# Second sequence's modulation rows, modulation sums and routing logits on TensorE: three small rearrangements in an adaptive-norm attention and expert kernel

## The chip, the cores and the metric

The kernel runs on one core of one Trainium2 chip. Its engines are TensorE (PE; PEld is its weight load), VectorE (DVE), ScalarE (ACT), GpSimd (POOL) and SyncE (SP), which issues most of the DMAs. Each works through its own queue in order. The metric is device time in microseconds, the median of three executions.

## The reference, cut to what matters

The input holds two sequences of 1024 tokens with 512 features. A vector c of each sequence makes six modulation rows; normed and modulated tokens go through an attention with cosine similarities, then through a top-2 mixture of eight experts with a shared expert.

```python
mod = (_silu(L0_c) @ L0_wmod).reshape(2, 6, 1, -1)
sa, ca, ga, sb, cb, gb = (mod[:, i] for i in range(6))
ga = (2 * (ga >= 0) - 1) * jnp.maximum(jnp.abs(ga), 0.25)   # gb alike
h = _layernorm(x) * (1 + ca) + sa
x = x + ga * attention(h)     # layernorm, K, V, rotary, A = sum(cos(K) * cos(V)), (A * Q) @ W_out
h = _layernorm(x) * (1 + cb) + sb
x = x + gb * moe(h)           # scores = softmax(h @ gate_w), the best 2 of 8, shared expert
```

## The kernel before, in words

All values are fp32. Tokens are taken in tiles of 128 rows: tiles 0 to 7 are the first sequence, 8 to 15 the second. Four tiles make a group; there are four groups.

**Modulation rows.** `c` is turned into four column pieces `sc_pad` (128 features by 32 columns, two of them used). `mod_parts(m, w, t)` multiplies each of the four pieces with its 128 rows of weight m, in four column tiles of the array, so that the four partial sums lie in partitions 0, 32, 64 and 96 of one PSUM bank, two rows each; a ScalarE copy brings the bank to SBUF. The partial sums are added by one more product with `pick`, a 128x2 matrix that has a one where a partition belongs to a sequence. `mod_sum` does that for both sequences at once, into two rows of a bank; `mod_add` then adds a constant, `mod_gate` makes the gate (sign and magnitude; two VectorE rows, one ScalarE row and one more VectorE row), and both store the rows in DRAM (`mods`), from where `spread` reads them into all partitions. `spread_now` instead multiplies with one column of `pick` broadcast to 128 columns, so that the row of one sequence comes out on all partitions at once, and ScalarE copies it. So `ca1[0]`, `sa[0]` (first sequence) and `ca1[1]`, `sa[1]` (second) are made. `turn_mod` transposes the rows of cb and sb into columns, `modT`, which `turn2` uses much later.

**The opening.** Three filler products (`turn_over(3, ones_row)`) run while the first weights land; then come the parts of ca and sa, their rows for the first sequence, and four more filler products `turn_over(4, parts_sa)` until the first tile is normed.

**The loop over tiles 0 to 7.** For each tile t: `norm1(t + 2)` norms a tile two ahead (`norm1_in`: moments `st_a`, `mv`, `sd_a`, `rs`; `norm1_mid` and `norm1_out`: two VectorE rows on `h`, which has one buffer; moments `st_b`, `mv_b`, `sd_b`, `rs_b`, `off_b`; ScalarE writes `hn`). `kv_half(t, 0)` multiplies K (four products into a bank, which VectorE adds a bias to), `turn1(t + 1)` transposes the next tile (`tr_a`) and ScalarE copies it in four pieces to `xnT`; then the steps in `side[t]` run, then `kv_half(t, 1)` multiplies V and `kv_back` computes the cosine sums (`sq` on ScalarE, `pr`, `inv`, `w` and `acc` on VectorE, the rotation on GpSimd). `side` spreads the rest of the modulation work and the transposes of W_q (`turn_wq`, four banks `wqT_0` to `wqT_3`) over the tiles:

```python
0: [second_rows],
2: [lambda: mod_gate(2, wm_ga), turn_wq],
4: [lambda: add(4, wm_cb, 1.0), lambda: add(3, wm_sb, 0.0)],
5: [lambda: own(5, wm_gb), lambda: turn_mod(0, raws[4])],
6: [lambda: mod_gate(5, wm_gb), lambda: turn_mod(1, raws[3])],
```

After the loop `mix` sums `acc` over the tokens (`amix`), and the second sequence's loop runs among the output projections of the first.

**The logits.** For each group, `logit_parts` multiplies the four pieces of the gate weights (32 columns each, eight used) with the transposed tokens in four column tiles, again with four partial sums in partitions 0, 32, 64 and 96. `route` then adds them: for each of the four token tiles a product with `pick_e` (128x8), 128 tokens by 8 experts, and one VectorE copy of 128x32 to SBUF. The softmax and the choice of two experts follow on VectorE and ScalarE; `place_rows` multiplies ranks from it.

**Order.** PSUM has eight banks: three buffers for products (`mm_ps`), two for transposes and small products (`tr_ps`), three for the shared expert (`sh_ps`). The source's order is a proposal: a scheduler settles the order of the instructions in each engine's queue by its own estimate of times. `tc.issue_after(x)` keeps what stands in it behind instruction x.

Of the kernel before, what the change touches and what calls it, by code (L numbers as in the profile page):

```python
# [8 lines left out]
FP = mybir.dt.float32  # L9
# [3 lines left out]
ALU = mybir.AluOpType  # L13
AX = mybir.AxisListType
# [4 lines left out]
P = 128  # L19
# [5 lines left out]
def kernel(  # L25
# [20 lines left out]
    nc = tc.nc  # L46
    B, S, D = x.shape
    E, _, H = w_gate.shape
    KC = D // P
    CT = P // KC  # L50
# [29 lines left out]
    const = ctx.enter_context(tc.tile_pool(name="const", bufs=1))  # L80
# [30 lines left out]
    ident = const.tile([P, P], FP, name="ident")  # L111
# [3 lines left out]
    ones_t = const.tile([P, P], FP, name="ones_t")  # L115
# [75 lines left out]
    wm_ga = load_mod(2, 3)  # L191
# [4 lines left out]
    wm_cb = load_mod(4, 4)  # L196
    wm_sb = load_mod(3, 5)
# [6 lines left out]
    wm_gb = load_mod(5, 0)  # L204
# [17 lines left out]
    silu = nc.vector.tensor_mul(sc_pad[:, :, 0:B], csb, sig_c)  # L222
    pick = late.tile([P, B], FP, name="pick")
    with tc.issue_after(silu.ins):
        nc.vector.tensor_reduce(
            pick, ident.rearrange("p (k c) -> p c k", k=KC)[:, 0:B, :], AX.X, ALU.add
        )
    pick_e = const.tile([P, E], FP, name="pick_e")
    with tc.issue_after(silu.ins):
        nc.vector.tensor_reduce(  # L230
            pick_e, ident.rearrange("p (k c) -> p c k", k=KC)[:, 0:E, :], AX.X, ALU.add
        )
    parts = {}

    copied = []
# [11 lines left out]
            )  # L247
        copied.append(nc.scalar.copy(t, ps))

    def mod_sum(m, w):  # L250
        ps = mm_ps(f"modsum_{m}")
        nc.tensor.matmul(ps[:B, :], pick, w[:, 0, :], start=True, stop=True)
        return ps[:B, :]


    def mod_add(m, w, plus):
        t = w[:B, 1, :]
        nc.vector.tensor_scalar(t, mod_sum(m, w), plus, None, ALU.add)
        nc.sync.dma_start(mods[m], t)
        return t  # L260

    def mod_gate(m, w):

        ps = mod_sum(m, w)
# [15 lines left out]
        mod_parts(m, w, t)  # L280
        return t

    def spread_now(t, b, plus, tag):
        ps = mm_ps(f"{tag}_{b}")
        nc.tensor.matmul(
            ps, pick[:, b : b + 1].to_broadcast([P, P]), t, start=True, stop=True
        )
        row = late.tile([P, D], FP, tag=tag, bufs=B, name=f"{tag}_{b}")
        nc.scalar.activation(row, ps, AF.Identity, bias=plus)
        return row  # L290

    modT = late.tile([P, 2, KC, B], FP, name="modT")

    def turn_mod(i, raw):
        ps = tr_ps(f"modT_{i}")
        for f in range(KC):
            nc.tensor.transpose(
                ps[:, f * B : (f + 1) * B], raw[:, f * P : (f + 1) * P], ident[0:B, 0:B]
            )
# [27 lines left out]
    def transposes(src, name):  # L327
        ps = tr_ps(f"tr_{name}")
        for f in range(KC):
            nc.tensor.transpose(  # L330
                ps[:, f * P : (f + 1) * P], src[:, f * P : (f + 1) * P], ident
            )
        return ps
# [7 lines left out]
    hn_of, turned1 = {}, {}  # L341
# [37 lines left out]
    def turn1(t):  # L379
        g, j = t // 4, t % 4  # L380
        hn = hn_of.pop(t)
        if j == 0:
            xnT[g] = act_tile(XNT_HOME[g], f"xnT_{g}")
        ps = transposes(hn, f"a{t}")
        for f in range(KC):
            turned1[t] = nc.scalar.activation(  # L386
                xnT[g][:, f, j * P : (j + 1) * P],
                ps[:, f * P : (f + 1) * P],
                AF.Identity,
                bias=colsb[:, 1, f : f + 1],  # L390
                scale=colsb[:, 0, f : f + 1],
            )
# [219 lines left out]
    rows = const.tile([P, NT, TOPK], I32, name="rows")  # L612
# [32 lines left out]
    def route(g, lgp):  # L645

        t0 = g * 4
        ps = tr_ps(f"lg_{g}")
        for j in range(4):
            nc.tensor.matmul(  # L650
                ps[:, j * E : (j + 1) * E],
                lgp[:, j * P : (j + 1) * P],
                pick_e,
                start=True,
                stop=True,
            )
        lg = small.tile([P, 4, E], FP, tag="lg", name=f"lgs_{g}")
        nc.vector.tensor_copy(lg.rearrange("p j e -> p (j e)"), ps[:, 0 : 4 * E])
        mx = small.tile([P, 4], FP, tag="mx", name=f"mx_{g}")
        nc.vector.tensor_reduce(mx, lg, AX.X, ALU.max)  # L660
        nc.vector.tensor_sub(lg, lg, mx.unsqueeze(2).to_broadcast([P, 4, E]))
        ex = small.tile([P, 4, E], FP, tag="ex", name=f"ex_{g}")
        nc.scalar.activation(ex, lg, AF.Exp)
        sm = small.tile([P, 4], FP, tag="sm", name=f"sm_{g}")
        nc.vector.tensor_reduce(sm, ex, AX.X, ALU.add)
        nc.vector.reciprocal(sm, sm)
        p = small.tile([P, 4, E], FP, tag="p", name=f"p_{g}")
        nc.vector.tensor_mul(p, ex, sm.unsqueeze(2).to_broadcast([P, 4, E]))
# [17 lines left out]
        both = small.tile([P, 4, E], FP, tag="both", name=f"both_{g}")  # L686
        nc.vector.tensor_add(both, pick[:, :, 0, :], pick[:, :, 1, :])
# [366 lines left out]
        return kvp.tile([P, D + 2 * R2], FP, tag="acc", bufs=1, name=f"acc_{b}")  # L1054

    def second_rows():
        ca1[1] = spread_now(parts_ca, 1, ones_t[:, 0:1], "ca1")
        sa[1] = spread_now(parts_sa, 1, zero_t, "sa")

    def own(m, w):  # L1060
        mod_parts(m, w, w[:, 0, :])

    raws = {}

    def add(m, w, plus):
        raws[m] = mod_add(m, w, plus)


    side = {
        0: [second_rows],  # L1070
        1: [lambda: own(2, wm_ga)],
        2: [lambda: mod_gate(2, wm_ga), turn_wq],
        3: [lambda: own(4, wm_cb), lambda: own(3, wm_sb)],
        4: [lambda: add(4, wm_cb, 1.0), lambda: add(3, wm_sb, 0.0)],
        5: [lambda: own(5, wm_gb), lambda: turn_mod(0, raws[4])],
        6: [lambda: mod_gate(5, wm_gb), lambda: turn_mod(1, raws[3])],
        7: [lambda: before_mix(0)],
    }
    turn_over(3, ones_row)
    parts_ca = own_parts(1, wm_ca)  # L1080
# [4 lines left out]
    parts_sa = own_parts(0, wm_sa)  # L1085
    norm1_mid(0)
    sa[0] = spread_now(parts_sa, 0, zero_t, "sa")
    turn_over(4, parts_sa)
    norm1_in(2)
    norm1_out(0)  # L1090
    norm1_mid(1)
    turn1(0)
    norm1_out(1)
    acc = start_acc(0)
    for t in range(NJ):
# [486 lines left out]
    sums = list(range(NT))  # L1582
# [106 lines left out]
```

## Time and profile before

| | |
|---|---|
| three executions | 773.6, 773.07, 772.42 us, median 773.07 |
| profiled execution | 773.89 us, span 772.0 us |
| busy: TensorE, VectorE, ScalarE, GpSimd | 754.5, 427.8, 233.3, 211.7 us |
| mean granted TensorE clock | 0.997 of full speed |

A row of the timeline has the start in microseconds from the span's beginning, the duration, engine, line and operation, the tensors written and read (buffer numbers left out), shapes, and the number of instructions merged; in brackets stands how long the engine had been idle and what ended it. A row of the waits has the engine and what it was about to do, whom it waited for, the total in microseconds, the number of times and the longest. An fp32 product of 512 columns appears as two records of 0.43 us spacing, a transpose of 128x128 as one.

### The profile page before, as it was taken

The page shows a single profiled execution, that of the slowest core. Times are in us where ns is not written, and L with a number is a line of the kernel's source. Part 1 is how long each engine was busy: PE and PEld are TensorE (multiplying, and loading weights), DVE is VectorE, ACT ScalarE, POOL GpSimd, SP SyncE. Part 2 cuts the span into 40 slices and gives each one's busy share as a digit, 9 for nine tenths or more (in the row PEclk, how much of TensorE's full clock was granted, in tenths as well). Part 3 has the DMA queues.
Part 4 walks back from the last instruction along what each step waited for, and adds up shares of the span by engine and source line. Part 5 has one row for each costly group of instructions (what it writes and reads, how often), then busy time and mean ns, then how long its engine had stood idle before and what let it go on. Part 6 is the DMA issues. An engine that isn't in the chain of part 4 may idle for free. (4 is left out here: it accounts for less than half of the span.)

```text
span 772.0 us, 8521 instructions
## 1 busy us (share of the span) xinstructions
PE 754.5 (98%) x2547; PEld 418.6 (54%) x2547; DVE 427.8 (55%) x980; ACT 233.3 (30%) x496; POOL 211.7 (27%) x241
## 2 busy tenths in 40 slices
PE   7999999999999999999999999999999998999997
PEld 2444444444444444584565656656656554888542
DVE  4888856898736888882221223222221121499964
ACT  4565523567542153110122111122111111122310
POOL 1234324754632686562100000000000000234530
PEclk9999999999999999999999999999999999999999
DMA  8951001312515611367999999999999885524551
GB/s 320 382 170 29 1 1 68 122 54 73 158 65 193 262 68 42 119 262 254 343 352 357 335 339 327 331 349 322 342 321 326 303 279 169 191 83 134 166 164 54
DMA packets 96368, 158.91 MB, mean 206 GB/s; under 512 B 8088, under 2 KB 51096, under 8 KB 96320
## 3 DMA queue, kind: packets, MB, share of 16 engines
q1 hardware_dynamic: 89984, 138.41, 53.3%
q0 software_dynamic: 5760, 18.88, 7.3%
q10 hardware_dynamic: 576, 1.05, 0.4%
q8 instruction: 22, 0.36, 0.2%
q14 instruction: 26, 0.21, 0.1%
HBM read 128.15 MB, written 30.16 MB: 205 GB/s over the span
## 5 line engine op out<-in xcount | busy, mean ns | idle before, releaser
L1341 POOL DMA_INDIRECT y<-ybuf,yrows x32 | 36.9, 1154 | 336.1 <-SPq L1567 287.0
L403 PE MATMUL kv<-w_kv,xnT 128*128 128x512 f32 x256 | 115.0, 596 | 0.5 <-ACT xnT L386 0.5
L1467 PE MATMUL by<-wd_r,gtT 128*128 128x512 f32 (+1 forms) x210 | 96.1, 593 | 0.9 <-DVEq L1559 0.9
L1439 PE MATMUL bg<-wg_r,hbT 128*128 128x352 f32 x280 | 88.9, 460 | 0.9 <-ACT y L1471 0.9
L1439 PE MATMUL bu<-wu_r,hbT 128*128 128x352 f32 x280 | 88.5, 459 | 0.0
L403 PEld LDWEIGHTS kv<-w_kv,xnT 128*128 128x128 f32 x256 | 47.0, 190 | 57.4 <-issue 49.0
L1439 PEld LDWEIGHTS bu<-wu_r,hbT 128*128 128x128 f32 x280 | 53.2, 190 | 29.6
L1454 DVE COPY gtT<-gtr 128x256 f32<-128x256 f32 x35 | 14.8, 424 | 97.0 <-PE gtr L1451 97.0
L1439 PEld LDWEIGHTS bg<-wg_r,hbT 128*128 128x128 f32 x280 | 50.4, 190 | 23.5 <-ACT y L1471 1.3
L564 PE MATMUL o<-wp,xnT 128*128 128x512 f32 x128 | 57.3, 593 | 0.0
L1318 DVE TENSOR_TENSOR sg_b<-sg_b,bg 128x352 f32<-128x352 f32 x35 | 18.2, 521 | 68.7 <-ACT sg_b L1317 68.7
L1467 PEld LDWEIGHTS by<-wd_r,gtT 128*128 128x128 f32 (+1 forms) x210 | 37.2, 191 | 34.6 <-issue 33.5
L1431 ACT COPY hbT<-tr_b 128x512 f32<-128x512 f32 x36 | 21.1, 585 | 101.2 <-PE tr_b L330 101.2
L1319 DVE TENSOR_TENSOR gt<-sg_b,bu 128x352 f32<-128x352 f32 x35 | 18.2, 521 | 47.2 <-PE bu L1439 47.2
L1471 ACT COPY y<-by 128x512 f32<-128x512 f32 x35 | 20.5, 587 | 70.8 <-PE by L1467 45.0
L564 PEld LDWEIGHTS o<-wp,xnT 128*128 128x128 f32 x128 | 23.9, 190 | 28.6 <-issue 27.0
L1317 ACT ACTIVATE sg_b<-bg 128x352 f32<-128x352 f32 x35 | 16.2, 463 | 76.1 <-PE bg L1439 76.1
L433 POOL TENSOR_TENSOR cross<-kv 128x128 f32<-128x128 f32 x16 | 12.6, 789 | 75.6 <-DVE kv L410 44.0
L426 ACT ACTIVATE sq<-kv 128x512 f32<-128x512 f32 x32 | 20.1, 630 | 31.1 <-DVE kv L410 26.7
L523 PE MATMUL wp<-aw,wqT 128*128 128x512 f32 x64 | 28.6, 597 | 0.9 <-DVE aw L504 0.7
L603 POOL TENSOR_TENSOR hr<-hr,cb 128x512 f32<-128x512 f32 x16 | 22.3, 1395 | 23.8 <-issue 13.2
L386 ACT ACTIVATE xnT<-tr_a,colsb 128x128 f32<-128x128 f32 x64 | 24.2, 456 | 14.2 <-PE tr_a L330 14.2
(320 smaller groups left out, 1269.2 us busy)
## 6 DMA issues: line engine op xcount, KB each, us to landing
wg_r<-in_w_gate_dram SPq DMA_DIRECT2D x35, 704.0 KB, 6.5
wu_r<-in_w_up_dram SPq DMA_DIRECT2D x35, 704.0 KB, 7.7
wd_r<-in_w_down_dram SPq DMA_DIRECT2D x35, 512.0 KB, 5.6
hb<-hbuf SPq DMA_DIRECT2D x36, 256.0 KB, 5.2
ybuf<-y SPq DMA_DIRECT2D x31, 256.0 KB, 5.4
wd_r<-in_w_down_dram SPq DMA_DIRECT2D x35, 192.0 KB, 5.6
wmod<-in_wmod_dram SPq DMA_DIRECT2D x6, 1024.0 KB, 10.5
x<-in_x_dram SPq DMA_DIRECT2D x3, 1024.0 KB, 10.5
```

The source lines that it names most:

```text
L386: turned1[t] = nc.scalar.activation(xnT[g][:, f, j * P : (j + 1) * P], ps[:, f * P : (f + 1) * P], AF.Identity, bias=colsb[:, 1, f : f + 1 ...
L403: nc.tensor.matmul(ps, xnT[g][:, k, j * P : (j + 1) * P], w_kv[:, i, k, :], start=(k == 0), stop=(k == KC - 1),)
L426: nc.scalar.activation(sq, kv[:, i, :], AF.Square, accum_out=ss[:, i : i + 1])
L523: nc.tensor.matmul(ps, wqT[:, k, f * P : (f + 1) * P], aw[:, k, :], start=(k == 0), stop=(k == KC - 1),)
L564: nc.tensor.matmul(ps, xnT[g][:, k, j * P : (j + 1) * P], wp[:, k, :], start=(k == 0), stop=(k == KC - 1),)
L603: nc.gpsimd.tensor_mul(h, h, cb1[b])
L1318: nc.vector.tensor_mul(sg[:m, :n], sg[:m, :n], pg[:m, :n])
L1341: nc.gpsimd.indirect_dma_start(out=y, out_offset=None, in_=ybuf, in_offset=bass.IndirectOffsetOnAxis(ap=yrows[:, t, s : s + 1], axis=0), b ...
L1431: nc.scalar.copy(hbT.rearrange("p k q -> p (k q)"), ps)
L1439: nc.tensor.matmul(ps[:, :H], hbT[:, k, :], wt[:, k, :], start=(k == 0), stop=(k == KC - 1))
L1467: nc.tensor.matmul(ps, gtT[:m, c, :], w[2][:m, c, :], start=(c == 0), stop=(c == NH - 1))
L1471: nc.scalar.copy(y, ps)
```

## The change

1. The products of the second sequence's rows `ca1[1]` and `sa[1]` move to the opening, in place of two of the four filler products; their copies on ScalarE are issued behind the last `xnT` copy of tile 0. `side[0]` becomes empty.
2. The sums of cb, sb and gb are multiplied in tile 5 into three column tiles of one bank (partitions 0, 32 and 64); the sum of ga stays alone in tile 2. The parts of gb move from tile 5 to tile 4, the gate of gb from tile 6 to tile 5, the stores of cb and sb from tile 4 to tile 5, the transpose of cb from tile 5 to tile 6.
3. The partial logits are transposed as they are, four 128x128 transposes for each group, and VectorE adds the four partial sums as it reads the bank. `pick_e` goes.

```diff
-    pick_e = const.tile([P, E], FP, name="pick_e")
...
-    def mod_sum(m, w):
-        ps = mm_ps(f"modsum_{m}")
-        nc.tensor.matmul(ps[:B, :], pick, w[:, 0, :], start=True, stop=True)
-        return ps[:B, :]
+    def mod_sums(*ws):
+        ps = mm_ps("modsums")
+        sums = []
+        for i, w in enumerate(ws):
+            rows = slice(i * CT, i * CT + B)
+            nc.tensor.matmul(
+                ps[rows, :], pick, w[:, 0, :], start=True, stop=True, tile_position=(0, i * CT)
+            )
+            sums.append(ps[rows, :])
+        return sums
...
-        ps = tr_ps(f"lg_{g}")
-        for j in range(4):
-            nc.tensor.matmul(
-                ps[:, j * E : (j + 1) * E],
-                lgp[:, j * P : (j + 1) * P],
-                pick_e,
-                start=True,
-                stop=True,
-            )
+        ps = transposes(lgp, f"lg{g}")
         lg = small.tile([P, 4, E], FP, tag="lg", name=f"lgs_{g}")
-        nc.vector.tensor_copy(lg.rearrange("p j e -> p (j e)"), ps[:, 0 : 4 * E])
+        nc.vector.tensor_reduce(
+            lg,
+            ps.rearrange("p (j k c) -> p j c k", j=4, k=KC)[:, :, 0:E, :],
+            AX.X,
+            ALU.add,
+        )
...
+    def first_gate():
+        mod_gate(2, wm_ga, *mod_sums(wm_ga))
+
+    def other_sums():
+        ws = (wm_cb, wm_sb, wm_gb)
+        cb, sb_, gb_ = mod_sums(*ws)
+        raws[4] = mod_add(4, wm_cb, cb, 1.0)
+        raws[3] = mod_add(3, wm_sb, sb_, 0.0)
+        mod_gate(5, wm_gb, gb_)
...
-        0: [second_rows],
+        0: [],
         1: [lambda: own(2, wm_ga)],
-        2: [lambda: mod_gate(2, wm_ga), turn_wq],
+        2: [first_gate, turn_wq],
         3: [lambda: own(4, wm_cb), lambda: own(3, wm_sb)],
-        4: [lambda: add(4, wm_cb, 1.0), lambda: add(3, wm_sb, 0.0)],
-        5: [lambda: own(5, wm_gb), lambda: turn_mod(0, raws[4])],
-        6: [lambda: mod_gate(5, wm_gb), lambda: turn_mod(1, raws[3])],
+        4: [lambda: own(5, wm_gb)],
+        5: [other_sums],
+        6: [lambda: turn_mod(0, raws[4]), lambda: turn_mod(1, raws[3])],
...
-    turn_over(4, parts_sa)
+    turn_over(2, parts_sa)
+    rows_1 = second_rows()
...
     turn1(0)
+    with tc.issue_after(turned1[0].ins):
+        ca1[1] = spread_copy(rows_1[0], 1, ones_t[:, 0:1], "ca1")
+        sa[1] = spread_copy(rows_1[1], 1, zero_t, "sa")
```

As the scheduler settles it, the order of TensorE changes little beside these places: in tile 0 the transposes of tile 1 come behind the first product of V, and in tile 6 the two groups of `modT` stand before and within the products of V. VectorE's and ScalarE's queues are in a different order through most of the loop over tiles 0 to 7: norm rows (`st_a`, `st_b`, `h`) stand later against the kv rows in tiles 0 to 3, and in ScalarE's queue `sd_b` of tile 4 stands between the first two and the last two `xnT` copies of tile 3.

More of the change, by code (lines that the diff above doesn't have):

```diff
@@ L227 @@
         )
-    pick_e = const.tile([P, E], FP, name="pick_e")
-    with tc.issue_after(silu.ins):
-        nc.vector.tensor_reduce(
-            pick_e, ident.rearrange("p (k c) -> p c k", k=KC)[:, 0:E, :], AX.X, ALU.add
-        )
     parts = {}
@@ L248, in mod_parts, with mod_add, mod_gate @@
         copied.append(nc.scalar.copy(t, ps))
-    def mod_sum(m, w):
-        ps = mm_ps(f"modsum_{m}")
-        nc.tensor.matmul(ps[:B, :], pick, w[:, 0, :], start=True, stop=True)
-        return ps[:B, :]
-    def mod_add(m, w, plus):
+    def mod_sums(*ws):
[8 more added lines that the diff above has]
+        return sums
+    def mod_add(m, w, ps, plus):
         t = w[:B, 1, :]
-        nc.vector.tensor_scalar(t, mod_sum(m, w), plus, None, ALU.add)
+        nc.vector.tensor_scalar(t, ps, plus, None, ALU.add)
         nc.sync.dma_start(mods[m], t)
         return t
-    def mod_gate(m, w):
-        ps = mod_sum(m, w)
+    def mod_gate(m, w, ps):
         t, mag = w[:B, 1, :], w[:B, 2, :]
@@ L281, in own_parts, with spread_product @@
         return t
-    def spread_now(t, b, plus, tag):
+    def spread_product(t, b, tag):
         ps = mm_ps(f"{tag}_{b}")
@@ L287, in spread_now, with spread_copy @@
         )
+        return ps
+    def spread_copy(ps, b, plus, tag):
         row = late.tile([P, D], FP, tag=tag, bufs=B, name=f"{tag}_{b}")
@@ L290, in spread_now @@
         return row
+    def spread_now(t, b, plus, tag):
+        return spread_copy(spread_product(t, b, tag), b, plus, tag)
     modT = late.tile([P, 2, KC, B], FP, name="modT")
@@ L647, in route @@
         t0 = g * 4
-        ps = tr_ps(f"lg_{g}")
-        for j in range(4):
-            nc.tensor.matmul(
-                ps[:, j * E : (j + 1) * E],
-                lgp[:, j * P : (j + 1) * P],
-                pick_e,
-                start=True,
-                stop=True,
-            )
-        lg = small.tile([P, 4, E], FP, tag="lg", name=f"lgs_{g}")
-        nc.vector.tensor_copy(lg.rearrange("p j e -> p (j e)"), ps[:, 0 : 4 * E])
+        ps = transposes(lgp, f"lg{g}")
+        lg = small.tile([P, 4, E], FP, tag="lg", name=f"lgs_{g}")
+        nc.vector.tensor_reduce(
[4 more added lines that the diff above has]
+        )
         mx = small.tile([P, 4], FP, tag="mx", name=f"mx_{g}")
@@ L1056, in second_rows @@
     def second_rows():
-        ca1[1] = spread_now(parts_ca, 1, ones_t[:, 0:1], "ca1")
-        sa[1] = spread_now(parts_sa, 1, zero_t, "sa")
+        return (
+            spread_product(parts_ca, 1, "ca1"),
+            spread_product(parts_sa, 1, "sa"),
+        )
     def own(m, w):
@@ L1063 @@
     raws = {}
-    def add(m, w, plus):
-        raws[m] = mod_add(m, w, plus)
+    def first_gate():
[6 more added lines that the diff above has]
+        mod_gate(5, wm_gb, gb_)
     side = {
-        0: [second_rows],
+        0: [],
         1: [lambda: own(2, wm_ga)],
-        2: [lambda: mod_gate(2, wm_ga), turn_wq],
+        2: [first_gate, turn_wq],
         3: [lambda: own(4, wm_cb), lambda: own(3, wm_sb)],
-        4: [lambda: add(4, wm_cb, 1.0), lambda: add(3, wm_sb, 0.0)],
-        5: [lambda: own(5, wm_gb), lambda: turn_mod(0, raws[4])],
-        6: [lambda: mod_gate(5, wm_gb), lambda: turn_mod(1, raws[3])],
+        4: [lambda: own(5, wm_gb)],
+        5: [other_sums],
+        6: [lambda: turn_mod(0, raws[4]), lambda: turn_mod(1, raws[3])],
         7: [lambda: before_mix(0)],
```

## The prediction

> **What bounds the kernel now.** I read the page first, for the engines' shares; then the waits of TensorE (PE), for what it waits on; then the busy time by stage; then the timeline at the three places that the diff touches.
>
> ```profile
> span 772.0 us, 8521 instructions
> PE 754.5 (98%) x2547; PEld 418.6 (54%) x2547; DVE 427.8 (55%) x980; ACT 233.3 (30%) x496; POOL 211.7 (27%) x241
> ```
>
> ```profile
> PE m L1012 <- ACTq L1567: 2.0, 1, 2.0
> ...
> PE rank L698 <- DVE both L687: 0.9, 1, 0.9
> ```
>
> ```profile
> 18.70:97.00 78.30, 78.26 (x247) 35.02 (x248) 68.12 (x158) 46.16 (x123) 28.57 (x42) 1.00 0.42 146
> ```
>
> PE is busy for 98% of the span, its longest wait is 2.0 us, and in the stage that projects the first sequence (18.70 to 97.00; columns after the length are PE, weight loads, VectorE, ScalarE, GpSimd, then granted clock and DMA) it idles for 0.04 us. So a microsecond of PE work taken out here is a microsecond gained, unless something else now ends last. VectorE has 68 of those 78 us filled: it is the engine to watch.
>
> **Part 1, the second sequence's rows.** Four filler products (`turn_over`) fill the wait for the first `hn`; two of them become the products of `ca1[1]` and `sa[1]`, of the same size, so the first 18.7 us stay as they are. In tile 0 the two products go:
>
> ```profile
> 22.27 0.60 PE L330 MATMUL tr_a<-ident,hn 128*128 128x128 f32 x4
> 22.71 1.02 PE L285 MATMUL ca<-parts,pick 128*128 128x512 f32 x2
> 23.57 1.02 PE L285 MATMUL sa<-parts,pick 128*128 128x512 f32 x2
> 24.43 7.03 PE L403 MATMUL kv<-w_kv,xnT 128*128 128x512 f32 x16
> ```
>
> From 22.71 to 24.43 that is 1.72 us of PE. But their two copies on ScalarE (0.57 us apart at 24.30 and 24.87) move forward to behind the first four `xnT` copies, ahead of `sd_b` of token tile 1, which stood at 20.09:
>
> ```profile
> 18.23 1.50 ACT L386 ACTIVATE xnT<-tr_a,colsb 128x128 f32<-128x128 f32 x4 [0.75 <-PE tr_a L330]
> ...
> 20.09 0.30 ACT L316 ACTIVATE sd_b<-mv_b,eps_t 128x1 f32<-128x1 f32 x1 [0.36 <-DVE mv_b L314]
> ...
> 20.87 0.81 ACT L325 ACTIVATE hn<-h,off_b,rs_b 128x512 f32<-128x512 f32 x1 [0.48 <-DVE off_b L324]
> ```
>
> So `sd_b` starts at 20.75 and `hn` of tile 1 ends at 22.34, not 21.68. PE is covered there: the new order puts one product of `kv_1` ahead of that transpose. What waits is VectorE: `h` of tile 2 needs the one h buffer that `hn` frees, and stands at the head of VectorE's queue. I carried the new order of VectorE on by the old rows' spacing (0.61 for an add, 0.77 for an `h`, 1.13 for a `cs` row): `hn` of tile 2 ends at 29.97 (was 29.23), while PE, 1.72 earlier, asks for it at 29.57: a wait of 0.45.
>
> The larger wait comes in tile 2. There the new ScalarE order puts `sd_b` of tile 4 between the two halves of the `xnT` copies of tile 3; in the old one that `sd_b` (39.15) was over before they began:
>
> ```profile
> 39.15 0.29 ACT L316 ACTIVATE sd_b<-mv_b,eps_t 128x1 f32<-128x1 f32 x1 [0.33 <-DVE mv_b L314]
> 39.79 0.60 PE L330 MATMUL tr_a<-ident,hn 128*128 128x128 f32 x4
> 40.97 1.48 ACT L386 ACTIVATE xnT<-tr_a,colsb 128x128 f32<-128x128 f32 x4
> 42.63 1.04 PE L490 MATMUL wqT<-ident,w_q 128*128 128x128 f32 x8
> ```
>
> PE now reaches this transpose at about 38.3 and the second group of `wqT` (42.63 before, 2.84 later) at 41.15. That group needs the bank that `xnT` of tile 3 frees. `mv_b` of tile 4 stands in VectorE's queue behind acc, h, st_b, st_a and two kv adds, and by the same spacing comes at 40.95, or 0.6 later if the h rows take 1.00 instead of 0.75 as they do beside GpSimd at 29.57. Then `sd_b`, the second half of `xnT`, and the bank is free at 42.2 to 42.9: a wait of 1.0 to 1.7, I take 1.2. Behind it the fourth `wqT` group waits 0.4 for a copy that now stands behind `hn` of tile 4. Part 1 by the sum: 1.72 - 0.45 - 1.2 - 0.4 = **0.3 us lost**, with ends at 1.7 gained (no wait) and 1.0 lost.
>
> **Part 2, the modulation sums.** Each sum of 2x512 takes one slot of a full product although it uses two columns:
>
> ```profile
> 59.52 0.60 PE L330 MATMUL tr_a<-ident,hn 128*128 128x128 f32 x4
> 60.05 1.88 PE L252 MATMUL modsum<-wmod,pick 128*2 128x512 f32 x4
> ...
> 69.36 1.06 PE L240 MATMUL mod<-wmod,sc_pad 128*32 128x512 f32 x8
> 70.36 0.41 PE L297 MATMUL modT<-ident,wmod 2*128 2x2 f32 x4
> ```
>
> Two sums hold PE from 60.05 to 61.86; four `mod` products side by side in column tiles take 69.36 to 70.36, 1.00. So three sums side by side cost 1.00, not 2.6. [...] The rows show the price: from a transpose to a tiled group 0.53 (68.83 to 69.36), to an untiled one 0.44 (22.27 to 22.71): 0.09 a change. [...] Tiles 4, 5 and 6 took 9.31, 8.83 and 8.79 from transpose to transpose; a tile without side work 7.31 (86.45 to 93.76). After: 3 x 7.31, plus 1.09 (`mod` of gb, a tile earlier), 1.09 (sums), 0.76 (two `modT`) = 24.87 against 26.93: 2.06. The second `modT` may wait 0.2 for the bank of `tr_a`; **1.9 us gained**.
>
> VectorE gets all five small rows (0.67 each, 0.41, 0.67: 3.1) in tile 5 instead of over two tiles. `hn` then comes some 2 us later but is wanted a whole tile later, and the kv banks have three buffers. Without that cover it would cost about 1.3. The two adds' DMAs (L259) move from 64 to about 72, the gate's (L270) from 82 to 73; on the SP queue the gate's store now stands ahead of the `sb` spread, which is wanted after 125. GpSimd's `ca1*ga` moves into a tile's rotation chain (1.26, delays acc once; PE is ten microseconds away). The mix at 97.63 had 0.4 us in hand; two small rows now stand in its chain: 0.1 lost.
>
> **Part 3, partial logits.** Four times:
>
> ```profile
> 163.14 0.60 PE L330 MATMUL tr_c<-ident,hr 128*128 128x128 f32 x4
> 163.58 0.96 PE L650 MATMUL lg<-pick_e,lgps 128*128 128x8 f32 x8
> 164.39 3.68 PE L833 MATMUL p<-hT,cg 128*128 128x512 f32 x8
> ```
>
> Four transposes take one pass each, 0.44; the four small products two passes with 128x128 weights, 0.81. 4 x 0.37 = 1.48. VectorE's copy (0.19) becomes a reduce of 128 elements: nearest rows are L718, 64 elements in 0.22, and L765, 128 in 0.28; from a bank I take 0.30, so +0.1 in each chain, bounded by 0 and 0.3. It matters only for group 2, whose rank product already waits 0.9 at 296.23: of its 0.37 about 0.2 stays. Nor does `choose(0)` lose: ScalarE saves a table load (1.28). **1.3 us gained.** The removed `pick_e` row (0.19 at 3.24) was followed by 3.86 idle: nothing.
>
> Sum: -0.3 + 1.9 - 0.1 + 1.3 = 2.8. The profiled execution took 773.89 (1.9 outside its span); 2.8 off is 771.1, and off the median, 773.07, **770.3**. Later stages move along: block 0's rows were asked for at 352.98, 16 us ahead of PE.
>
> [...] Tile 2's waits lie among 16 transposes. [...] The stage's clock column is 1.00 with the same transposes in it, products stand between the waits, and I take the trace.
>
> **Rivals.** (a) No wait forms, VectorE is ahead of my spacing: 1.72 + 2.06 + 1.48 = 5.26, 767.8. For it: before, every wait here was under 0.1. Against: the `hn` lead at tile 2 was only 2.1. Chance 0.2. (b) The forecast, 0.48. (c) The sums of two columns do not run side by side: 1.6 less, 771.9; no two-column row shows it. 0.1. (d) Slower: the norm's lead does not come back. In tile 3 `hn` ends 0.85 ahead of its transpose, before 4.4. If VectorE needs over 7.3 us for a tile, each of six transposes (tiles 4 to 9) waits about 1 us: 6 + 2.05 against 5.26 is 2.8 lost, 775.9. It decides once VectorE is 0.85 later than I have it at tile 3. Against: in 86.45 to 93.76 VectorE is busy 5.67 of 7.31; for: 8.46 of 9.31 in tile 4. 0.12. (e) Some other wait eats one or two more: about 772. 0.1.
>
> **Numbers.** About 0.2%, 1.5 us, can be told from no change. Faster needs below 771.5: (a), (b) but for its tail, part of (c): 0.70. Within 0.2%: 0.18. Slower: 0.12. The range from 767.9 to 773.0 leaves out (d) and the far end of (a).
>
> **What would show it.** Right: no `ca`/`sa` products after `kv`; three sums within 1.0; `lg` gone for 0.44 transposes; a PE wait over 0.8 at a `wqT` row, released by an `xnT` copy. Wrong: no such wait (a), sums one after another (c), or `tr_a` waiting for `hn` in tiles 4 to 9 (d).

## The result, and the profile after

| | before | after |
|---|---|---|
| median, both measured side by side (9 executions each) | 773.07 us (772.42 to 775.12) | 769.99 us (768.9 to 772.12) |
| profiled execution, span | 773.89, 772.0 us | 772.12, 770.3 us |

The ratio of after to before is 0.996, with an interval of 0.9945 to 0.9974: 3.1 us less. The forecast was 770.3. The sum came out right; its terms did not, as the two stages show. In the profiled executions the way from the first `tr_a` to the first output projection `o` took 97.15 us before and takes 97.90 after: it is 0.75 longer, although 3.8 us of products were taken out of it (1.72 and 2.06 by the prediction's count). The way from there to `count`, the end of the routing, took 199.56 and takes 197.01. All that the profiled execution gained comes from the logits.

The page of the changed kernel, its first line of engines, and two lines of TensorE's waits (what it was about to do, whom it waited for, total, times, longest):

```profile
PE 751.9 (98%) x2527; PEld 415.8 (54%) x2527; DVE 428.7 (56%) x979; ACT 232.5 (30%) x495; POOL 214.9 (28%) x241
```

```profile
PE m L1016 <- ACTq L1586: 2.0, 1, 2.0
...
PE amix L474 <- DVE acc L471: 1.3, 1, 1.3
```

The shares are those of before. The second wait shown is new: it stands at the mix, where I had forecast 0.1. The timeline at the places that the prediction named, first tile 2 and then tile 5 (start, duration, engine, line, tensors; in brackets the idle time before it and what ended it):

```profile
41.98 1.13 PE L497 MATMUL wqT<-ident,w_q 128*128 128x128 f32 x8 [0.48 <-ACT xnT L393]
...
44.32 0.66 PE L497 MATMUL wqT<-ident,w_q 128*128 128x128 f32 x4 [0.35 <-ACT wqT L500]
```

```profile
68.35 1.03 PE L251 MATMUL modsums<-wmod,pick 128*2 128x512 f32 x6
69.31 3.27 PE L410 MATMUL kv<-w_kv,xnT 128*128 128x512 f32 x7
```

The two waits in tile 2 are where they were forecast, released by the rows that were named, and half as long. The three sums do run side by side: 0.96 us from their start to the next product. At the mix:

```profile
97.29 1.05 PE L474 MATMUL amix<-ones_t,acc 128*128 128x1 f32 x8 [1.30 <-DVE acc L471]
98.21 0.64 PE L337 MATMUL tr_a<-ident,hn 128*128 128x128 f32 x4
99.24 4.97 PE L530 MATMUL wp<-aw,wqT 128*128 128x512 f32 x7 [0.39 <-DVE aw L511]
```

The busy time by stage (length; PE, weight loads, VectorE, ScalarE, GpSimd with their instructions; granted clock, DMA share, GB/s) tells who is late, and what the wait sets off:

```profile
68.80:77.70 8.90, 8.90 (x32) 4.09 (x27) 8.44 (x19) 4.94 (x14) 3.08 (x6) 1.00 0.18 47
77.70:86.50 8.80, 8.80 (x28) 4.15 (x27) 8.61 (x22) 5.42 (x16) 5.36 (x8) 1.00 0.05 15
86.50:97.60 11.10, 9.80 (x29) 4.38 (x27) 10.51 (x26) 6.02 (x17) 4.75 (x7) 1.00 0.00 1
...
100.00:104.00 4.00, 4.00 (x7) 1.59 (x6) 3.54 (x7) 2.30 (x6) 1.63 (x2) 0.63 0.00 0
```

VectorE is occupied for 27.56 of these first 28.80 us (in the same stretches before: 7.06, 7.92 and 8.62, together 23.60); rows beside GpSimd rows are counted at the length they have there (`pr` 1.00 at 84.17, beside `cross`; 0.68 at 84.59 before). Counted from the first `tr_a`, TensorE would have been at the mix 1.84 us earlier than before, and VectorE's last row for it is only 0.18 earlier: TensorE gives the lead back there. Then the granted clock is 0.63 from 100 to 104, where it was 1.00 before. The trace's record of the clock has one stretch at half, from 99.6 to 103.0, that before does not have; `amix` to the first `o` takes 18.34 us in place of 17.05.

### The profile page after: what moved, and what is told of

The parts are those of the page before. It is cut to its first block, busy times and chain, and to the rows that moved or that the text cites. A ratio compares the mean times of both kernels' runs of the same rounds, so it can differ in the third digit from the quotient of the medians.

```text
span 770.3 us, 8477 instructions
## 1 busy us (share of the span) xinstructions
PE 751.9 (98%) x2527; PEld 415.8 (54%) x2527; DVE 428.7 (56%) x979; ACT 232.5 (30%) x495; POOL 214.9 (28%) x241
```

## The experiments

All are timed against the kernel before in the same rounds. "Opening to `o`" is the way from the first `tr_a` to the first `o` of the profiled execution. The last column counts the executions with a mean granted clock of 0.999 or more, of 0.996 to 0.998, and of 0.995 or less. In all 14 profiles these go with no stretch at half clock, with one, and with two or more (one at the very end, which every profile has, is left out); I take the other executions the same way. The mean does not tell where a stretch lies.

| kernel | median us (before beside it) | ratio, interval | wait at the mix | opening to `o` | executions with no, one, more half-clock stretches, by mean clock |
|---|---|---|---|---|---|
| before | | | under 0.1 | 97.15 | 28, 38, 0 |
| after | 769.99 (773.07) | 0.996, 0.9945 to 0.9974 | 1.30 | 97.90 | 3, 3, 3 |
| rows_only | 775.89 (773.79) | 1.002, 1.0007 to 1.0032 | 1.21 | 99.60 | 2, 3, 7 |
| sums_only | 773.77 (773.79) | 0.9994, 0.9983 to 1.0006 | 0.60 | 97.88 | 3, 4, 5 |
| logits_only | 770.78 (773.79) | 0.996, 0.9945 to 0.9974 | none | 98.87 | 3, 2, 1 |
| early_sums | 771.15 (773.79) | 0.997, 0.9954 to 0.9986 | 2.12 | 100.08 | 2, 3, 3 |
| fill_mix | 770.74 (774.04) | 0.9961, 0.9948 to 0.9974 | filled | 96.71 | 1, 4, 0 |
| pin_tile2 | 770.90 (774.04) | 0.9962, 0.9948 to 0.9976 | 1.3 | 97.26 | 2, 3, 2 |
| gate_late | 768.47 (774.04) | 0.9942, 0.9929 to 0.9955 | 0.56 | 95.96 | 4, 1, 0 |
| adds_on_act | 770.43 (774.04) | 0.996, 0.9948 to 0.9973 | 1.20 | 97.80 | 1, 4, 2 |
| gate_early | 767.60 (773.53) | 0.9924, 0.9909 to 0.9938 | none | 95.19 | 6, 0, 0 |
| all_three | 768.52 (773.53) | 0.9938, 0.9922 to 0.9955 | filled | 95.47 | 3, 3, 0 |
| before_wait | 776.16 (773.53) | 1.004, 1.0026 to 1.0053 | 1.93 | 101.68 | 0, 5, 5 |
| gate_after_mix | 769.66 (773.92) | 0.9949, 0.9931 to 0.9966 | none | 95.52 | 1, 5, 1 |

### The three parts alone

`rows_only`, on the kernel before:

```diff
-    turn_over(4, parts_sa)
+    turn_over(2, parts_sa)
+    rows_1 = second_rows()
...
+    with tc.issue_after(turned1[0].ins):
+        ca1[1] = spread_copy(rows_1[0], 1, ones_t[:, 0:1], "ca1")
+        sa[1] = spread_copy(rows_1[1], 1, zero_t, "sa")
...
-        0: [second_rows],
+        0: [],
```

> The kernel before with part 1 alone (the second sequence's rows at the opening). My sum with the waits that the trace after shows in tile 2: 1.72 of products out of tile 0, less 0.2 at the opening and 0.48 + 0.35 at wqT, so about 0.7 us faster, 772.4, and tr_a of tile 5 about 0.7 earlier than before. The mix should wait no more than the 0.1 of before if its wait of 1.30 comes from the lumped sums; the rival, that a TensorE moved forward by any cause outruns VectorE at the mix, gives a wait of 0.5 or more here and a gain near 0.

`sums_only`, on the kernel before:

```diff
+        ws = (wm_cb, wm_sb, wm_gb)
+        cb, sb_, gb_ = mod_sums(*ws)
...
-        4: [lambda: add(4, wm_cb, 1.0), lambda: add(3, wm_sb, 0.0)],
-        5: [lambda: own(5, wm_gb), lambda: turn_mod(0, raws[4])],
-        6: [lambda: mod_gate(5, wm_gb), lambda: turn_mod(1, raws[3])],
+        4: [lambda: own(5, wm_gb)],
+        5: [other_sums],
+        6: [lambda: turn_mod(0, raws[4]), lambda: turn_mod(1, raws[3])],
```

> The kernel before with part 2 alone (sums of three rows side by side in tile 5, the gate's row moved with them). If the lumping in tile 5 puts VectorE behind: 2.06 saved at the sums, then a wait of 1.0 to 1.4 at the mix for the last piece of acc, so 0.7 to 1.0 us faster, 772.2, and less in runs whose granted clock falls at the mix. The rival, that the wait at the mix needs part 1 as well, gives 1.9 faster, 771.2, and a wait under 0.3.

`logits_only`, on the kernel before:

```diff
-        ps = tr_ps(f"lg_{g}")
...
+        ps = transposes(lgp, f"lg{g}")
...
-        nc.vector.tensor_copy(lg.rearrange("p j e -> p (j e)"), ps[:, 0 : 4 * E])
+        nc.vector.tensor_reduce(
+            lg,
+            ps.rearrange("p (j k c) -> p j c k", j=4, k=KC)[:, :, 0:E, :],
+            AX.X,
+            ALU.add,
+        )
```

> The kernel before with part 3 alone (partial logits turned). By my prediction's sum 1.3 us faster, 771.8; by the trace after, in which the wait of 0.89 before the rank product of group 2 has gone too, 2.0 to 2.4 faster, 770.9. Nothing changes before 160 us: no wait at the mix and no stretch of half clock near 100 us by either.

The mix's line in TensorE's timeline, first of `rows_only`, then of `sums_only`:

```profile
98.50 1.05 PE L473 MATMUL amix<-ones_t,acc 128*128 128x1 f32 x8 [1.21 <-DVE acc L470]
```

```profile
96.70 1.05 PE L473 MATMUL amix<-ones_t,acc 128*128 128x1 f32 x8 [0.60 <-DVE acc L470]
```

By the medians the rows alone lose 2.1 us where I expected 0.7 gained, the sums alone change nothing that can be told, and the logits alone bring 3.0. These add up to 0.9, and the three together bring 3.1: the parts are not additive. Up to the transposes of tile 9 they are (0.42 and 1.51 gained alone, 2.00 together), but each of the first two, run alone, pays a wait at the mix and a half clock behind it (granted clock 0.66 and 0.65 from 100 to 104; 2.9 and 2.2 us together), and together they pay these once (2.75). The first of my two readings of the mix, that the lumped sums cause its wait, falls as the only cause: the rows make a wait of 1.21 without any lumping. The sums alone make one of 0.60, half of what I expected. The rival named for `rows_only` holds, and the time is worse than it said. The profiled execution of `logits_only` has a half-clock stretch of its own, from 19.3 to 22.7 (`kv` from 18.75 takes 5.40 for eight records, 3.70 before), which makes its way to `o` 1.72 longer; nothing of the change stands there, and what sets it off is open. From `o` to `count` it takes 197.03, the 2.5 us of the whole change.

### Is it the lumped rows?

```diff
-        3: [lambda: own(4, wm_cb), lambda: own(3, wm_sb)],
-        4: [lambda: own(5, wm_gb)],
-        5: [other_sums],
-        6: [lambda: turn_mod(0, raws[4]), lambda: turn_mod(1, raws[3])],
+        3: [lambda: own(4, wm_cb), lambda: own(3, wm_sb), lambda: own(5, wm_gb)],
+        4: [other_sums],
+        5: [lambda: turn_mod(0, raws[4])],
+        6: [lambda: turn_mod(1, raws[3])],
```

> The changed kernel with the three sums (and the gate's own row before them) one tile earlier, in tile 4, so that the VectorE rows that follow them have one tile more to be caught up with before the mix. If the mix waits because VectorE has not made good these rows by tile 9, the wait falls from 1.30 to under 0.5, the half clock after it goes, and the time is 1 to 2.5 us below the changed kernel's, about 768.5. The rival, that VectorE runs behind TensorE in tiles 7 to 9 whatever comes before (its own work per tile as long as TensorE's), leaves the wait at 1.0 or more and the time where it is.

```profile
97.89 1.73 PE L474 MATMUL amix<-ones_t,acc 128*128 128x1 f32 x8 [2.12 <-DVE acc L471]
```

The wait grew. With a tile more to catch up, VectorE did not: its last three `acc` rows begin at 80.13, 87.92 and 95.78, 7.8 us apart, while TensorE takes 7.31 for a tile without side work. The rival holds: what VectorE loses in tile 4 is still lost at the mix. No `acc` row takes more than 1.02 in this kernel. What is held up is an `h` row of VectorE beside a GpSimd row of the attention gate, 1.85 in place of 0.75 (more on these rows below). So the wait at the mix needs no long `acc` row.

### The clock

The changed kernel, `fill_mix`:

```diff
+FILL = 2
...
+        if b == 0:
+            warm = mm_ps("warm")
+            for _ in range(FILL):
+                nc.tensor.matmul(warm, ones_t, w_o[:, 0, :], start=True, stop=True)
         ps = tr_ps(f"amix_{b}")
```

> The changed kernel with two further 128x512 products, whose result nobody reads, on TensorE ahead of the mix's products, where it waits 1.30 us for acc. They do not bring acc sooner. If TensorE's idle time with the tiny products behind it is what lets the granted clock fall to half at 99.6 to 103.0, the half-clock stretch near the mix goes, wp to the first o takes 15.2 instead of 16.4, and the median falls by up to 1.2 us (the slow levels of the runs thin out). The rival, that the clock falls for another reason (a fixed rhythm, or the products' 128x1 shape), leaves a half-clock stretch near 100 us in the profile and the time unchanged or up to 0.5 longer.

Its timeline at the mix, and the stage behind it:

```profile
95.54 1.88 PE L476 MATMUL warm<-w_o,ones_t 128*128 128x512 f32 x4
97.26 0.95 PE L479 MATMUL amix<-ones_t,acc 128*128 128x1 f32 x8
```

```profile
100.00:104.00 4.00, 4.00 (x11) 1.85 (x10) 3.89 (x8) 1.62 (x5) 0.99 (x2) 1.00 0.00 0
```

The half clock at the mix is gone (1.00 where it was 0.63), and `amix` to `o` takes 16.90 in place of 18.34. `wp` to the first `o` takes 14.70, even less than expected. In the median it does not show: four of five executions still had one half-clock stretch (mean clock 0.997; 1.0 in the fifth). In the profiled one it begins at about 654, where the wait of 2.0 for `m` ends; before has that one too, in its own profile at 658.2.

The other direction, `before_wait`, on the kernel before:

```diff
-        nc.vector.tensor_add(half[:, 0, :], pair[:, :, 0], pair[:, :, 1])
+        for _ in range(7 if b == 0 else 1):
+            nc.vector.tensor_add(half[:, 0, :], pair[:, :, 0], pair[:, :, 1])
```

> The kernel before, untouched by any of the three parts, with six further VectorE rows (128x128, the same sum written again, about 0.21 each) ahead of the mix: acc is ready 1.3 later and TensorE waits 1.3 to 1.4 there. If a wait of that size is enough for the clock, part of the runs (a third to three quarters) fall to 0.995 and a half-clock stretch of 3.4 lies behind the mix in those, so the median is 1.3 to 3 us above before. If the half clock needed something of the change itself, every run is 1.3 above before and none is at 0.995.

The wait came out longer than meant, 1.93, since one of VectorE's `kv` rows (0.68) came to stand among the last rows for the mix. Five of ten executions are at 0.994 or less; the profiled one has half clock from 99.6 to 106.5. Its median is 2.6 above before. So nothing of the change itself is needed: a wait of 1.93 at this place is enough in half of the executions.

### The wqT waits of tile 2

```diff
+        elif t == 2:
+            norm1_first(t + 2)
         else:
             norm1(t + 2)
         kv_half(t, 0)
         turn1(t + 1)
+        if t == 2:
+            norm1_last(t + 2)
```

> The changed kernel with the second half of tile 4's norm put behind tile 3's xnT rows on ScalarE, so that sd_b of tile 4 no longer stands between the two halves of xnT. The waits of 0.48 and 0.35 at the wqT groups go if sd_b's place is their cause, and tr_a of tile 4 comes 0.8 earlier. If VectorE decides when acc is ready, as I now think, nothing of it arrives at the mix (its wait grows by as much, to about 2.1) and the time stays within 0.3 of the changed kernel's; if TensorE decides, the time is 0.8 less.

The wait of 0.48 for `xnT` goes, so `sd_b`'s place was its cause; but the one of 0.35 for the copy of `wqT` becomes 0.8. From the first `tr_a` to that of tile 4 it is 32.08 in place of 32.24, and the mix waits 1.28. The time is the changed kernel's. I had expected `tr_a` 0.8 earlier; with 0.16 the kernel does not tell which engine decides.

### Where VectorE loses its microsecond

All `acc` rows of the first sequence take 1.00 to 1.02, except one. GpSimd's row and VectorE's in the changed kernel, then the same two before:

```profile
61.97 1.26 POOL L1055 TENSOR_TENSOR sa<-b_o,sa 128x512 f32<-128x512 f32 x1
...
62.04 2.00 DVE L458 SCALAR_TENSOR_TENSOR acc<-pr,w,acc 128x768 f32<-128x768 f32 x1 [0.64 <-POOL pr L444]
```

```profile
58.18 1.27 POOL L1051 TENSOR_TENSOR sa<-b_o,sa 128x512 f32<-128x512 f32 x1 [0.68 <-issue]
...
62.56 1.02 DVE L451 SCALAR_TENSOR_TENSOR acc<-pr,w,acc 128x768 f32<-128x768 f32 x1 [0.79 <-POOL pr L437]
```

Before, GpSimd had done its two gate rows (`ca` times `ga`, `b_o` plus `sa`) when tile 4's rotation began. They were not free there: the first stands beside an `h` row of VectorE that takes 1.85 in place of 0.75.

```profile
56.19 1.85 DVE L361 SCALAR_TENSOR_TENSOR h<-h,rs,sa 128x512 f32<-128x512 f32 x1
```

```profile
56.23 1.26 POOL L1050 TENSOR_TENSOR ca<-ca,ga 128x512 f32<-128x512 f32 x1 [4.50 <-DVE h L355]
```

Part 1 shifts the norm, and the scheduler's order puts the gate rows into the rotation. The first then delays `pr`, for which `acc` waits; the second begins 0.07 us ahead of `acc`, and `acc` ends 0.8 after it, at 64.04. `rows_only` has the same row at 2.00; in `sums_only` all take 1.0, and the `h` row takes 1.86 as before.

`gate_late`, the changed kernel with the two rows behind tile 5's:

```diff
+        def gates():
+            nc.gpsimd.tensor_mul(cg[b], ca1[b], ga[b])
+            nc.gpsimd.tensor_add(sg[b], b_o, sa[b])
+
+        if b == 0:
+            with tc.issue_after(rotated[4].ins):
+                gates()
+        else:
+            gates()
```

Here `rotated[4]` is tile 4's last GpSimd row; the scheduler went one tile further.

> The changed kernel with the two GpSimd rows of the attention gate (ca times ga, b_o plus sa, 1.26 us each) put behind tile 5's GpSimd rows. In the changed kernel they stand among tile 4's, and the acc row of tile 4 takes 2.00 beside one of them where it took 1.02 before. If this collision, caused by part 1's shift of tile 4, is what puts VectorE behind, acc of tile 4 takes 1.02 again, the wait at the mix falls from 1.30 to under 0.6 and the time by 0.7 or more. The rival, that a VectorE which is busy 92% of tiles 5 to 9 makes its own pace, leaves the wait at 1.0 or more.

```profile
61.06 1.00 DVE L458 SCALAR_TENSOR_TENSOR acc<-pr,w,acc 128x768 f32<-128x768 f32 x1
...
68.85 2.01 DVE L458 SCALAR_TENSOR_TENSOR acc<-pr,w,acc 128x768 f32<-128x768 f32 x1
```

```profile
68.77 1.27 POOL L1055 TENSOR_TENSOR ca<-ca,ga 128x512 f32<-128x512 f32 x1
```

`acc` of tile 4 is back at 1.00, and the collision has moved to tile 5's: 0.08 ahead of it stands the other row of the pair. Even so the last `acc` begins 0.76 earlier (counted from the first `tr_a`), and the mix waits 0.56. `pr` of tile 4 is no longer delayed; a held row is still there. The profile has no half-clock stretch at the mix, and four of the five executions have none anywhere (mean clock 0.999). This is the fastest kernel here that keeps the computation. Against before it is 4.5 us less by the ratio; its interval overlaps that of the changed kernel, so that it beats this one is likely and not shown.

`adds_on_act` takes work from VectorE instead:

```diff
-        nc.vector.tensor_scalar(t, ps, plus, None, ALU.add)
+        nc.scalar.activation(t, ps, AF.Copy, bias=plus)
```

> The changed kernel with the two bias adds that follow the sums (2x512 each, 0.67 us each on VectorE) on ScalarE, which is busy about half of these tiles. If VectorE sets when acc is ready, 1.3 us less work in tile 5 brings acc 0.8 to 1.3 sooner, the wait at the mix falls to 0.5 or less and the half clock behind it goes in most runs: 1 to 2.5 us less than the changed kernel. The rival, that the round trip of the norm between VectorE and ScalarE (h cannot be overwritten before hn has read it) sets the pace, leaves the wait at 1.0 or more, or lengthens it, as the rows now stand in ScalarE's queue.

```profile
73.02 0.69 DVE L267 TENSOR_SCALAR wmod<-modsums 2x512 f32<-2x512 f32 x1 [0.98 <-ACT wmod L260]
```

The wait stays at 1.20. VectorE does 1.3 less, but its next row in order, the first of the gate of gb, now waits 0.98 for the two adds on ScalarE (L260, 71.81 to 72.99), and the `h` row behind it waits 0.63 for an `hn` that ScalarE does after them. The experiment tells less than it should: it gave back what it took, and does not weigh VectorE's load against the norm's round trip.

`gate_early` puts the two rows ahead of tile 4's. In this kernel and in `all_three` they also stand ahead of the norm of tile 7, which then reads rows that are gated already: that part of the computation is changed, and the time is that of an order which the data do not allow.

```diff
+    def gate_rows(b):
+        ga[b] = spread(2, b, late, "ga", 1)
+        cg[b], sg[b] = ca1[b], sa[b]
+        nc.gpsimd.tensor_mul(cg[b], ca1[b], ga[b])
+        nc.gpsimd.tensor_add(sg[b], b_o, sa[b])
...
-        4: [lambda: own(5, wm_gb)],
+        4: [lambda: own(5, wm_gb), lambda: gate_rows(0)],
```

> The changed kernel with the two 1.26 us gate rows of GpSimd ahead of tile 4's GpSimd rows, in the place that they had before, so that neither runs where an acc row begins. My theory now: a VectorE row that begins while a GpSimd row of 128x512 runs goes on until that row is over (acc 2.00 instead of 1.02), and VectorE, which is full from tile 5 on, never makes this up. Then all acc rows take 1.0, acc is ready 1.0 to 1.8 earlier than in the changed kernel, the mix waits under 0.4, and the time is 768.0 to 768.6. The rival, that the GpSimd rows of tile 4 come 1.8 later instead and acc waits for pr just as long, leaves the wait at 1.0 or more.

All `acc` rows take 1.0, the mix does not wait, and the way to `o` is 2.7 shorter than in the changed kernel: 1.45 ahead of the mix and 1.26 behind it, where the half clock is gone. None of the six executions has a half-clock stretch (mean clock 0.999 or 1.0), not even at the wait for `m`; why that one is missing too is open. The median is 0.4 below the lower end of what I expected.

`all_three` adds the edit of `pin_tile2` and one unread product ahead of the mix:

```diff
+        elif t == 2:
+            norm1_first(t + 2)
...
+        if t == 2:
+            norm1_last(t + 2)
...
+        if b == 0:
+            warm = mm_ps("warm")
+            nc.tensor.matmul(warm, ones_t, w_o[:, 0, :], start=True, stop=True)
```

> The kernel of gate_early with tile 4's norm behind the xnT rows in tile 2 and one unread 128x512 product ahead of the mix. If the mix no longer waits once the GpSimd rows are out of the way, the 0.25 to 0.5 of tile 2 arrives at the end and the product costs up to its 0.45: 767.8 to 768.5. If VectorE still sets the mix, it equals gate_early within 0.2.

At 768.52 its median is 0.9 above `gate_early`, but three of its six executions have a half-clock stretch (mean clock 0.997); the three without take 767.6 to 767.85, as long as `gate_early`. The wait in tile 2 did not go: the copy of `wqT` now costs 0.85, and `tr_a` of tile 4 stands where it was (49.63 and 49.62). The product costs 0.86 ahead of the mix, twice what I had said, since the place it filled is no longer empty; of that, 0.28 is left at `o`.

`gate_after_mix`, the changed kernel with the rows held back until `acc` is finished:

```diff
+        first = nc.gpsimd.tensor_copy(seen_acc, behind[:, 0:1])
+        with tc.issue_after(first.ins):
+            nc.gpsimd.tensor_mul(cg[b], ca1[b], ga[b])
+            nc.gpsimd.tensor_add(sg[b], b_o, sa[b])
...
     aT = mix(0, acc)
+    gate_rows(0, acc)
```

> The changed kernel with the two gate rows of GpSimd behind the mix: a GpSimd copy of one column of the finished acc holds them back until VectorE's last row for the mix is through. No acc row of the first sequence then begins beside a 1.26 us GpSimd row. By the theory that these meetings and nothing else put VectorE behind, all acc rows take 1.0, the mix waits under 0.3, no half-clock stretch follows, and the time is near that of gate_early, 767.5 to 768.3. The price can come behind the mix: if the rows that scale w_o (0.60 each on VectorE, on the way to wp) are held by the GpSimd rows beside them, wp to the first o is 1 to 2 us longer and the time 768.5 to 770.

```profile
95.60 1.00 PE L474 MATMUL amix<-ones_t,acc 128*128 128x1 f32 x8
...
98.33 2.84 PE L530 MATMUL wp<-aw,wqT 128*128 128x512 f32 x6 [1.24 <-DVE aw L511]
```

```profile
96.74 1.26 POOL L1059 TENSOR_TENSOR sa<-b_o,sa 128x512 f32<-128x512 f32 x1
```

```profile
96.83 2.10 DVE L511 TENSOR_SCALAR aw<-w_o,aT 128x512 f32<-128x512 f32 x2
```

The first half of the expectation came, and it is the test that counts, since this kernel keeps the computation: the mix does not wait, with every `acc` at 1.0, the last row for it is 1.53 earlier than in the changed kernel, no half clock follows, and the way to `o` is 2.38 shorter. The two rows that scale `w_o` take 2.10 together (1.20 in the changed kernel), since the first again begins 0.09 behind a GpSimd row, and `wp` waits 1.24 for it. But the way to `o` is only 0.33 longer than in `gate_early`, not 1 to 2. The rest of the distance to `gate_early` in the median (769.66 against 767.60) is a half-clock stretch: six of the seven executions have one or more (mean clock 0.994 to 0.997), in the profiled one it begins at about 653, at the wait for `m`, and the single one without took 767.66.

## Why the prediction was right in its sum and wrong in its parts

The forecast was 2.8 us less, 3.1 were measured. Of the first stage the sum had said 1.5 gained (-0.3 + 1.9 - 0.1); the profiled execution lost 0.75. Of the logits it had said 1.3; they brought 2.5. Two errors of opposite sign met; that the sum hit was luck, and the time alone would have confirmed the working. Term by term, from `tr_a` to `tr_a` in the two profiled executions:

- **Part 1, tile 0 to 3: -0.3 forecast, 0.40 gained.** The way to `tr_a` of tile 3 is 1.49 shorter (1.72 of products forecast). The wait of 0.45 at tile 2 did not form: `hn` kept the forecast time, but TensorE arrived 0.4 later than I had it, at 29.95, just as `hn` ended; half of that is an opening that began 0.2 later. The waits at `wqT` were forecast at 1.2 and 0.4 and measured 0.48 and 0.35. The mechanism of the first was right, `pin_tile2` shows it, and its size was 2.5 times too large.
- **Part 2, tiles 4 to 8: 1.9 forecast (2.06 less a possible wait), 1.60 gained.** The three sums cost 1.15 with their surroundings (1.09 forecast); the two `modT` cost 1.06 (0.76 forecast), `mod` of gb 1.19 (1.09). Rival (c) is out: columns of two rows run side by side, three sums in 0.96.
- **The mix: 0.1 forecast, 1.46 lost.** This is the step that failed. I had written that GpSimd's row "delays acc once; PE is ten microseconds away". The rows (I had thought of one, there are two) delay `acc` of tile 4 by 1.74, not by 1.26: against `gate_after_mix`, counted from the first `tr_a`, it begins 0.74 later because `pr` is late, and then takes 1.0 longer. Of these 1.74, 1.53 are still there at the last row for the mix, which is where TensorE asks for `acc`: VectorE has almost nothing to make them good with. Before, it lost 1.1 to the same rows, but TensorE came 1.84 later and `acc` was ready 0.4 ahead of it. I had noted 68 of 78 us for VectorE in this stage, called it "the engine to watch", reckoned with `h` rows made longer by GpSimd in tile 2, and then costed this delay by TensorE's distance instead of VectorE's slack. Rival (d) named the right engine and the wrong place: the transposes of tiles 4 to 9 never wait, and the lag is paid once, at the mix.
- **The clock: 0 forecast, 1.29 lost between `amix` and `o` in the profiled execution.** I took the stage's clock column of before, 1.00, and at tile 2 it stayed at 1.00 (40 to 50). At the mix it fell, to 0.63 from 100 to 104: there a wait of 1.30, eight small products and four transposes follow each other. The record of the clock shows stretches of 3.413 us, and the one at the mix begins 27 such lengths after the record does. All seven kernels that wait 0.6 or more there have a half-clock stretch behind it in their profile, beginning 0.2 to 2.8 us after `amix` (granted clock from 100 to 104: 0.66 in `rows_only`, 0.65 in `sums_only`, 0.71 in `adds_on_act`, 0.50 in `early_sums` and `before_wait`); none of the other seven has. Counted by the mean clock as in the table, 27 of the 65 executions of those seven kernels have two or more, and 2 of the 101 of the others. Not every execution pays: 13 of the 65 have no stretch at all, three of the changed kernel's nine among them. What decides it from one execution to the next is not shown.
- **Part 3: 1.3 forecast, 2.5 gained.** The four transposes save what was said: they take 0.43 for a group where the products took 0.81. The wait of 0.89 at group 2's rank product, which I let absorb part of it, has gone altogether. The rows of VectorE and of GpSimd there, before:

```profile
293.10 1.14 DVE L668 TENSOR_TENSOR p<-ex,sm 128x32 f32<-128x32 f32 x1
```

```profile
292.92 1.26 POOL L604 TENSOR_TENSOR hr<-hr,sb 128x512 f32<-128x512 f32 x1
```

and after:

```profile
292.73 0.27 DVE L672 TENSOR_TENSOR p<-ex,sm 128x32 f32<-128x32 f32 x1
```

```profile
293.02 1.27 POOL L611 TENSOR_TENSOR hr<-hr,sb 128x512 f32<-128x512 f32 x1
```

A row of 128x32 took 1.14 us: it began inside a GpSimd row and ended with it (294.24 and 294.18). After the change it is over 0.02 before that GpSimd row begins. Some 0.9 us of the gain (1.14 less 0.27) is this meeting that no longer takes place; it fell out of the new order by chance, I had not seen it. `logits_only` has no rank wait either; `rows_only` and `sums_only`, which leave the logits as they were, keep it at 0.9.

So the whole: 0.40 + 1.60 - 1.46 - 1.29 = -0.75 for the first stage, 2.55 for the second, 1.8 in the profiled execution. That execution has two half-clock stretches, at the mix and at about 656; the median one, by its mean clock of 0.997, has one, which fits the 1.3 more that make 3.1. What stays open is what sets VectorE's pace of 7.0 to 7.7 us in the last tiles before the mix: its own load, the norm's round trip with ScalarE over the one `h` buffer, or GpSimd's rotation rows, beside which `pr`, `h` and `w` take 1.00, 0.92 and 0.41 after (at 84.17 to 86.43) and 0.68, 0.75 and 0.27 before (at 82.72 to 86.19). `adds_on_act` did not part them, and a second `h` buffer was not tried. In `gate_after_mix` these rows are just as long and the mix does not wait, so the gate rows are enough to make the difference in the changed kernel.

## What to carry to other kernels

A delay is paid where the next engine asks for the result of the delayed one (here 1.53 of 1.74 us, at the mix), so cost it by the slack of the engine that is delayed, up to the first place where the two meet, and not by the distance to the engine that bounds the kernel. Before an order is moved, look at which GpSimd rows come to stand beside VectorE rows on its critical chain: here two rows of 1.26 us decided over 2.4 us on the way to `o`. And after a prediction that hits the time, run the parts alone: this one hit with one part that loses by itself, one that does nothing and one that brings nearly all.

## What the runs showed of the hardware that I had not expected

- Some VectorE rows that read two tensors from SBUF and began within 0.2 us of a GpSimd row's start took longer, and ended after that row: `acc` 2.00 (the changed kernel) and 2.01 (`gate_late`) in place of 1.02, `h` 1.85 in place of 0.75 and `p` 1.14 in place of 0.27 (both before). They ended 0.81, 0.82, 0.55 and 0.06 us after it. (The recorded start of that `h` is 0.04 ahead of the GpSimd row's, so a gap this small does not tell which goes first.) A GpSimd row took longer too: the second gate row in `gate_late`, beginning at 70.00 while `acc` runs to 70.86, takes 1.98 in place of 1.26. `aw` in `gate_after_mix`, which reads one tensor and a scalar of each partition, took 1.45 in place of 0.60 beside a GpSimd row; the `wmod` rows of VectorE that read PSUM with a constant keep 0.67 to 0.69 beside that gate row of `gate_late`. What parts the rows that take longer from those that do not is not shown.
- A wait of TensorE at the mix of 0.6 to 2.1 us, shorter than the 3.41 us of a half-clock stretch, with eight small products and four transposes behind it, had one or two such stretches behind it in the profiles: `amix` to `o` is 0.8 to 1.5 us longer than before's 17.05 with one (`pin_tile2`, `rows_only`) and 2.4 to 2.5 with two (`before_wait`, `early_sums`). The profile of `gate_late`, with a wait of 0.56, has none (granted clock 1.00 from 93 to 104).
